# Moving one layer's weight sums out of an attention stage and into the feed-forward stage beside it

## The chip, the core and the metric

The kernel runs on one core of a Trainium2 chip. The time is device microseconds (us) of one execution. A core has a matrix engine (TensorE, in the profile PE, with PEld for its weight loads), three engines for elementwise work (VectorE as DVE, ScalarE as ACT, GpSimd as POOL), an engine that here only issues transfers (SyncE, SP), and 16 DMA engines that move data between the chip's main memory (DRAM) and the on-chip memory (SBUF). TensorE writes into PSUM, a separate memory of eight banks. Each engine runs its own instructions strictly in order, and so does each queue of transfers that an engine issues: an instruction that waits holds up all that stands behind it.

## What is computed

The input x has two batches of 2048 tokens of 256 features. The output is x plus an attention plus a feed-forward network (FFN), both on the same normalized input:

```
xn  = layernorm(x)
q, k, v = xn Wq, xn Wk, xn Wv                      # all 256 -> 256
att = softmax(causal(q k^T) / 16) v Wo
h   = silu((xn w1^T) * w1_s) * ((xn w2^T) * w2_s)  # 256 -> 1024
h   = gelu((h h1^T) * h1_s)                        # 1024 -> 1024
h   = gelu((h h2^T) * h2_s)                        # 1024 -> 1024
out = x + att + (h w3^T) * w3_s                    # 1024 -> 256
```

The FFN weights w1, w2, h1, h2 and w3 hold only -1, 0 and 1 in the test's data, and everything is float32.

## The kernel before

**Two stages.** The attention of all tokens comes first, and then the FFN of all tokens. The tokens are cut into eight blocks n of 512, four to a batch. The FFN reads the normalized input, turned so that the features lie on the partitions, from DRAM (xT_d), where the attention stage has put it, and the attention's result from DRAM too (r_d).

**The attention.** A query tile (n, t) is 128 tokens. There are 32 tiles, numbered j = 0 to 31: batch 0 from its last tile (which looks at all 2048 keys) to its first, then batch 1 from its first tile to its last. For precision, each float32 operand is held as a rounded part and a remainder, and a product takes three matmuls. For each block of 512 keys, `score` does 6 matmuls (line 345); VectorE copies the scores out of PSUM and takes their maximum (the scale-and-max instruction, and `low`, line 360); ScalarE takes the exponentials of the whole row (L366). The exponentials have to be turned before they can be multiplied with the values. Short rows are turned by TensorE (`pt`, L410). Long rows are turned "by blocks": VectorE turns 32x32 squares (L236), SyncE's queue stores them to a scratch in DRAM (`d`, L241) and loads them back rearranged (`e`, L248). Then ScalarE rounds them (`pT`, L404), VectorE or GpSimd makes the remainder (L406), and `weigh` multiplies with the values (`po`, L424 and L429).

**The order of the attention.** The program's order is written out by hand. `merged(a, b, beside)` (L43) interleaves two lists of steps, the scores of tile j and the weighing of an earlier tile, by their costs, which are counted in columns that TensorE passes. A row that is turned by blocks is weighed at the earliest 42,000 such columns after its scores (DELAY_BLOCKS), another one 9,000 after. After each step `merged` calls `beside(cost)` (L565), which takes the next piece of background work from a queue once enough columns have passed.

**The background work.** The FFN has a fast path that holds only if the weights are what they are in this data. In it the 1024 x 1024 layers h1 and h2 are computed as 2 x 2 blocks with seven block products in place of eight (the list STEPS), and so need, for each layer, seven weight matrices of 512 x 512: the quarters A11, A12, A22 and four sums S1 to S4. These are made during the attention and put in DRAM (`factors`), and at the same time it is found out whether the weights have the values that the path needs. There are two kinds of background work:

- *Looks* (`look`, L487) at w1, w2 and w3, six in all, of 512 KB each: a load issued by ScalarE, for w1 and w2 a rounding by GpSimd into SBUF, then VectorE masks the low bits and ScalarE sums them into a column of `low_bits`. One is taken before every second tile from j = 3 on.
- *Rounds of factors* (the queue `factoring`, L510 to L560), from tile j = 14 on (FACTORS_FROM), so from shortly before the second batch: four for h1 and four for h2. A round loads two 512 KB chunks c and c+4 of the weight (ScalarE's queue, L521), takes the sign of each (ScalarE, L527), counts where the chunk differs from its sign (VectorE, L529), makes four sums of 128 x 512 (GpSimd, L539), and stores A11, the four sums and A12, A22 (SyncE's queue, L550 to L553, 1.75 MB in all).

The signs and the sums lie in the tile xh0 (1 MB), which is the place of the FFN's first input and is unused until then. So a round's first sign can be written only once the store of the last round's sums has left xh0, and the FFN's first input is loaded (L663, on SyncE's queue) only after the last store. The chunks share two staging buffers (`stgp`).

When the queue is empty, VectorE takes the maximum of `low_bits` (L657), TensorE and VectorE make the flag of it, and after the attention all engines read the flag and take the branch to `ffn_ternary` (L665), or to a slower FFN that holds for all weights.

**The FFN.** It takes the blocks in four pairs (n, n+1). `first(n)` (L696) computes the gated layer: for each of 16 parts of 128 x 512, 8 matmuls (L709), four into each of two banks, a silu by ScalarE into a tile `a` (L714), and a product by VectorE (L716) into `f`. It goes through the quarters B11, B12, B22, B21 and, with `split` (L692 and L693), `t1` and `b22`, makes the right-hand sides of the seven products. `square` does the seven products of a layer (L756), each of 32 matmuls into four banks, after loading their left factor from DRAM (L749, SyncE's queue, three buffers). In the end comes w3 (L847). GpSimd has in this stage one subtraction per part in `b22` (L734), one in `square` (L791) and the sum of x and the attention's result (L837). w3 is loaded at the start of the FFN (L820) and rounded by GpSimd (L131). The banks of PSUM (eight) and the buffers of the pools `raw` (26 of 128 x 512) and `h` (16) are taken in turns.

The functions that the change touches:

Of the kernel before, what the change touches and what calls it, by code (L numbers as in the profile page):

```python
# [32 lines left out]
FACTORS_FROM = 14  # L33
# [29 lines left out]
def attn_ffn_kernel(  # L63
# [72 lines left out]
    def rows(n, t):  # L136
        return ds((n % NB) * TB + t * P, P)

    with ExitStack() as actx:
# [342 lines left out]

        low_bits = cp.tile([P, 32], F32, name="low_bits")
        looked = [0]
        looks = []

        def look(src, dst):  # L487
            def go():
                t = stgp.tile([P, SC], F32, tag="stg", name=f"stg_{looked[0]}")
                nc.scalar.dma_start(out=t, in_=src)  # L490
                if dst is not None:
                    rounded(dst, t)
                tb = t.bitcast(U32)
                with tc.issue_after(marks["DVE"]):
                    nc.vector.tensor_scalar(tb, tb, LOW_BITS, None, ALU.bitwise_and)
                at = low_bits[:, looked[0] : looked[0] + 1]
                nc.scalar.activation(t, tb, AF.Copy, accum_out=at)
                looked[0] += 1

            looks.append(go)  # L500

        for src, dst in ((w1, w1_sb), (w2, w2_sb)):
            for c in range(src.shape[1]):
                look(src[:, c, :], dst[:, c, :])
        for c in range(0, HC, SC // D):
            look(w3[:, c : c + SC // D, :].rearrange("p c d -> p (c d)"), None)

        factoring = []  # L510

        def factor(name, src, c):

            halves = []
            sums = xh0.rearrange("p c h t -> p (c h) t")
            f = factors[name]

            def fetch():
                for k in (c, c + HK):
                    t = stgp.tile([P, SC], F32, tag="stg", name=f"stg_{name}_{k}")  # L520
                    nc.scalar.dma_start(out=t, in_=src[:, k, :])  # L521
                    halves.append(t)

            def compare(i):
                t, sign = halves[i], sums[:, ts(i, 2), :].rearrange("p a o -> p (a o)")
                with tc.issue_after(marks["ACT"]):
                    nc.scalar.activation(sign, t, AF.Sign)  # L527
                with tc.issue_after(marks["DVE"]):
                    nc.vector.scalar_tensor_tensor(  # L529
                        sign, t, 1.0, sign.bitcast(F32), ALU.mult, ALU.not_equal,  # L530
                        accum_out=low_bits[:, looked[0] : looked[0] + 1],
                    )
                looked[0] += 1

            def of(i):
                return halves[i // 2][:, ts(i % 2, HB)]

            def add(out, x, y, op):
                nc.gpsimd.tensor_tensor(sums[:, out, :], x, y, op)  # L539

            def s12():
                add(0, of(1), of(3), ALU.add)
                add(1, sums[:, 0, :].bitcast(F32), of(0), ALU.subtract)

            def s43():
                add(2, of(2), sums[:, 1, :].bitcast(F32), ALU.subtract)
                add(3, of(0), of(1), ALU.subtract)

            def store():
                nc.sync.dma_start(out=f[:, 0, c, :], in_=of(0))  # L550
                nc.sync.dma_start(out=f[:, 1:5, c, :], in_=sums.bitcast(F32))
                nc.sync.dma_start(out=f[:, 5, c, :], in_=of(2))
                nc.sync.dma_start(out=f[:, 6, c, :], in_=of(3))  # L553

            factoring.extend([
                (6000, fetch), (9500, lambda: compare(0)), (2500, lambda: compare(1)),
                (3000, s12), (3000, s43), (3000, store),
            ])

        for name, src in (("h1", h1), ("h2", h2)):  # L560
            for c in range(HK):
                factor(name, src, c)
        since = [0]

        def beside(cost):  # L565
            if j >= FACTORS_FROM:
                since[0] += cost
                if factoring and since[0] >= factoring[0][0]:
                    since[0] = 0
                    factoring.pop(0)[1]()  # L570
# [43 lines left out]
        def before(j):  # L614
# [12 lines left out]
            if j >= 3 and j % 2 and looks:  # L627
                looks.pop(0)()
# [6 lines left out]
        while until < len(tiles) - 1:  # L635
# [17 lines left out]
            if not factoring and not checked:  # L653
                assert not looks
# [10 lines left out]
    def ffn_ternary(actx):  # L665
# [4 lines left out]
        rawp = actx.enter_context(tc.tile_pool(name="rawpt", bufs=26))  # L670
        hp = actx.enter_context(tc.tile_pool(name="hpt", bufs=4 * HK))
        tp = actx.enter_context(tc.tile_pool(name="tpt", bufs=2))
# [23 lines left out]
        def first(n):  # L696
# [3 lines left out]
            for k in ("B11", "B12", "B22", "B21"):  # L700
                xh = xh1 if k[2] == "2" else xh0
                for i in range(HK):
# [3 lines left out]
                    for p, w in ((p1, w1_sb), (p2, w2_sb)):  # L706
# [6 lines left out]
                    g = tp.tile([P, TB], F32, tag="a", name=f"a_{name}")  # L713
                    nc.scalar.activation(g, p1, AF.Silu, scale=sc["w1"][:, o : o + 1])  # L714
                    f = B[k][i] = raw(f"f_{name}")
                    nc.vector.scalar_tensor_tensor(  # L716
                        f, p2, sc["w2"][:, o : o + 1], g, ALU.mult, ALU.mult
# [5 lines left out]
                    elif k == "B22":  # L723
                        b22(B, sets, f"{n}", i)
            return B, sets
# [14 lines left out]
        def square(layer, n, B, sets, last):  # L740
# [5 lines left out]
            def product(step, out, start):  # L746
# [6 lines left out]
                for o in range(HK):  # L753
                    for c in range(HK):
                        for a in range(2):
# [4 lines left out]
                            )  # L760

# [54 lines left out]

        load_xh(1)
        for c in range(0, HC, SC // D):
            t = fw.tile([P, SC], F32, name=f"stgt_{c}")
# [231 lines left out]
```

## Time and profile before

The median of three runs is 897.68 us (897.17 to 897.79). The profiled execution took 901.06 us, of which its span is 899.3 us.

| | busy us | share of the span | instructions |
|---|---|---|---|
| TensorE (PE) | 860.9 | 96% | 4280 |
| VectorE (DVE) | 615.8 | 68% | 1111 |
| ScalarE (ACT) | 498.6 | 55% | 881 |
| GpSimd (POOL) | 257.6 | 29% | 192 |

The DMA engines moved 158.33 MB, 176 GB/s on the mean. The mean granted clock of TensorE was 0.983 of full speed.

The attention runs from 0 to about 303.9 us, the FFN from there to the end. The batches change at about 150 us. A line of the timeline has a start, a duration, the engine, the line of the kernel, the operation, its output and inputs by the program's names, the shapes, and in brackets for how long the engine stood idle before it and what it had waited for. A line of a table by stage has the stretch, its length, then for PE, PEld, DVE, ACT and POOL the busy time and the number of instructions, then the granted clock, the share of the DMA engines' time that was busy, and GB/s. A line of the waits has the engine and instruction that waited, what it waited for, the sum of those waits, their number and the longest.

### The profile page before, as it was taken

To read this page: it belongs to the slowest core of one execution; us is meant where nothing else is said; L and a number is where in the kernel's file an instruction comes from. 1 tells how busy PE (TensorE), PEld (TensorE's weight loads), DVE (VectorE), ACT (ScalarE), POOL (GpSimd) and SP (SyncE) were. 2 spreads that over 40 slices of the span, in tenths; PEclk is the share of its full clock that TensorE was granted. 3 is DMA by queue.
4 is the path that set the end of the run, shared out by engine and by line. 5 is a ranking of instruction groups with operands and counts; after the bars stand their busy time and mean duration, and the time that the engine had idled before them with its cause. 6 is when DMAs were issued, how large, how long until landed. Compare 5 with 4: busy or idle time off the path is not lost.

```text
span 899.3 us, 12302 instructions
## 1 busy us (share of the span) xinstructions
PE 860.9 (96%) x4280; PEld 725.0 (81%) x4280; DVE 615.8 (68%) x1111; ACT 498.6 (55%) x881; POOL 257.6 (29%) x192
## 2 busy tenths in 40 slices
PE   8999999889886899999999999999999999999996
PEld 5988878778674788888988888898888898888886
DVE  6698566777675396596479487649659647948763
ACT  3456465545444356576446576726658644656670
POOL 4022533534346242150026024014315002602401
PEclk8999999999996999999999999999999999999999
DMA  7686698688987754444433444442444443144412
GB/s 251 246 243 203 160 329 290 222 283 291 323 272 242 275 200 153 154 154 141 141 94 141 140 141 141 144 145 90 145 153 154 153 141 95 48 140 141 141 48 74
DMA packets 62838, 158.33 MB, mean 176 GB/s; under 512 B 6576, under 2 KB 36400, under 8 KB 53552
## 3 DMA queue, kind: packets, MB, share of 16 engines
q1 hardware_dynamic: 59024, 144.87, 47.6%
q10 hardware_dynamic: 3744, 12.58, 4.5%
q8 instruction: 36, 0.59, 0.3%
q14 instruction: 34, 0.28, 0.1%
HBM read 109.72 MB, written 47.71 MB: 175 GB/s over the span
## 4 chain that ended last, share of the span: by engine, by line
PE 68%; DMA 16%; POOL 5%; DVE 5%; ACT 2%; SPq 2%; issue 2%; ACTq 0%; POOLq 0%; DVEq 0%
PE ps_h_X L756 26%; PE ps_w_B L709 13%; PE ps_h_Z L756 13%; PE ps_h_Y L756 6%; PE ps_y L847 6%; DMA factors_h<-xh 5%; DMA e<-d 4%; DMA d<-b 4%; POOL xh L539 3%; SPq L248 2%; PE pv L317 1%; PE pss L345 1%; DMA x<-d_x 1%; POOL pT L406 1%; DVE st L219 1%
## 5 line engine op out<-in xcount | busy, mean ns | idle before, releaser
L345 PE MATMUL pss<-k,q 128*128 128x512 f32 (+3 forms) x480 | 110.9, 372 | 3.0 <-DVE q L196 2.1
L345 PEld LDWEIGHTS pss<-k,q 128*128 128x128 f32 x480 | 82.9, 191 | 17.2 <-DVE q L196 2.6
L424 PE MATMUL po<-v,pT 128*128 128x512 f32 x272 | 81.0, 411 | 11.0 <-ACT pT L404 8.8
L756 PE MATMUL ps_h_X<-h_h_T,w_h_S 128*128 128x512 f32 x384 | 89.0, 389 | 0.0
L756 PEld LDWEIGHTS ps_h_X<-h_h_T,w_h_S 128*128 128x128 f32 x384 | 72.1, 188 | 15.0
L837 POOL TENSOR_TENSOR rt<-rt,xt 128x1024 f32<-128x1024 f32 x8 | 19.2, 2400 | 222.7 <-DMA rt<-r_d 203.6
L714 ACT ACTIVATE a_w_B<-ps_w_B,w_s_sb 128x512 f32<-128x512 f32 x64 | 43.1, 684 | 46.8 <-PE ps_w_B L709 44.6
L775 ACT ACTIVATE k_h_u<-k_h_u,h_s_sb 128x512 f32<-128x512 f32 x64 | 46.3, 723 | 40.8 <-DVE k_h_u L774 40.6
L734 POOL TENSOR_TENSOR k_h_u<-k_h_p,k_h_u 128x512 f32<-128x512 f32 x16 | 23.2, 1452 | 147.4 <-ACT h_h_B L692 130.8
L424 PEld LDWEIGHTS po<-v,pT 128*128 128x128 f32 x272 | 48.5, 195 | 19.5 <-ACT pT L404 10.3
L709 PE MATMUL ps_w_B<-xh,w_sb 128*128 128x512 f32 x256 | 61.3, 398 | 2.8 <-DMA xh<-xT_d 2.8
L366 ACT ACTIVATE s<-s,low 128x1024 f32<-128x1024 f32 (+7 forms) x48 | 42.9, 896 | 36.0 <-DVE low L360 34.2
L847 PEld LDWEIGHTS ps_y<-w_sbt,h_h_B 128*128 128x128 f32 x512 | 62.0, 192 | 0.3
L847 PE MATMUL ps_y<-w_sbt,h_h_B 128*128 128x256 f32 x512 | 62.1, 283 | 0.0
L709 PE MATMUL ps_w_B<-xh1t,w_sb 128*128 128x512 f32 x256 | 60.6, 396 | 0.0
L709 PEld LDWEIGHTS ps_w_B<-xh,w_sb 128*128 128x128 f32 x256 | 48.9, 192 | 13.4 <-issue 3.0
L756 PE MATMUL ps_h_Y<-h_h_B,w_h_A 128*128 128x512 f32 x256 | 59.3, 389 | 0.0
L756 PE MATMUL ps_h_X<-h_h_T,w_h_A 128*128 128x512 f32 x256 | 59.3, 389 | 0.0
L406 POOL TENSOR_TENSOR pT<-e,pT 128x512 fp32r<-128x512 f32 (+3 forms) x30 | 35.5, 1185 | 77.6 <-ACT pT L404 68.0
L709 PEld LDWEIGHTS ps_w_B<-xh1t,w_sb 128*128 128x128 f32 x256 | 48.2, 188 | 11.7
L756 PEld LDWEIGHTS ps_h_Y<-h_h_B,w_h_A 128*128 128x128 f32 x256 | 48.0, 188 | 10.0
L756 PEld LDWEIGHTS ps_h_X<-h_h_T,w_h_A 128*128 128x128 f32 x256 | 48.0, 188 | 10.0
(135 smaller groups left out, 1865.7 us busy)
## 6 DMA issues: line engine op xcount, KB each, us to landing
w_h_S<-factors_h SPq DMA_DIRECT2D x32, 1024.0 KB, 4.8
w_h_A<-factors_h SPq DMA_DIRECT2D x24, 1024.0 KB, 4.8
d<-b SPq DMA_DIRECT2D x18, 512.0 KB, 3.9
e<-d SPq DMA_DIRECT2D x72, 128.0 KB, 4.4
xT_d<-k SPq DMA_DIRECT2D x8, 1024.0 KB, 4.9
stg_h<-in_ffn_h_w ACTq DMA_DIRECT2D x16, 512.0 KB, 6.5
factors_h<-xh SPq DMA_DIRECT2D x8, 1024.0 KB, 8.3
factors_h<-stg_h SPq DMA_DIRECT2D x24, 256.0 KB, 5.1
```

The lines of the kernel that those rows point to most:

```text
L345: nc.tensor.matmul(out=ps[:, :w], lhsT=qs[n][:, c, a, ts(t, P)], rhs=ks[m][:, c, b, :w], start=(k == 0), stop=(m < n and k == 3 * DC - 1),)
L366: marks["ACT"] = nc.scalar.activation(st["s"][:, at], st["s"][:, at], AF.Exp, bias=low, accum_out=st["sums"][:, u // UK : u // UK + 1],).ins
L406: engine.tensor_tensor(lo, src, hi.bitcast(F32), ALU.subtract)
L424: nc.tensor.matmul(out=st["po"], lhsT=pT[:, 0, ts(j, P)], rhs=vs[m][:, j, :, :], start=(m == first and j == 0), stop=False,)
L539: nc.gpsimd.tensor_tensor(sums[:, out, :], x, y, op)
L709: nc.tensor.matmul(out=p, lhsT=w[:, c, ts(o, P)], rhs=xh[:, c, a, :], start=(c == 0 and a == 0), stop=(c == DC - 1 and a == 1),)
L714: nc.scalar.activation(g, p1, AF.Silu, scale=sc["w1"][:, o : o + 1])
L734: nc.gpsimd.tensor_tensor(B["B12"][i], B["B22"][i], B["B12"][i], ALU.subtract)
L756: nc.tensor.matmul(out=out[o], lhsT=w[:, c, ts(o, P)], rhs=sets[right][c][:, a, :], start=(start and c == 0 and a == 0), stop=(c == HK - 1 ...
L775: nc.scalar.activation(C[k][o], r[o] if r else banks[o], AF.Gelu, scale=s[:, at : at + 1])
L837: nc.gpsimd.tensor_tensor(rest, rest, xt, ALU.add)
L847: nc.tensor.matmul(out=ys[t][:, :D], lhsT=h[c][:, a, ts(t, P)], rhs=w3_sb[:, c, :], start=(c == 0 and a == 0), stop=(c == HC - 1 and a == 1),)
```

## The change

The sums of h1 are made in the attention as before. The sums of h2 are made in the FFN beside the first pair of blocks. All comparisons, those of h2 too, stay in the attention, since the flag depends on them.

- One queue `looks` takes the place of the two kinds of background work. It is emptied through `beside` from tile j = 3 on (LOOKS_FROM). Its order: four looks at w1 and w2; then four times a round for h1 (two loads, two comparisons, four sums, the stores) and two comparisons for h2 without sums or stores; then two looks at w3. In TensorE columns it is 330,000 long, in 56 steps. The store of the sums is issued ahead of those of the quarters.
- In the FFN a list `later` holds four `make_h2(c)` and two `load_w3`. `make_h2` loads two chunks of h2 again (SyncE's queue), makes four sums on GpSimd in a tile of its own, and issues four stores. The four are taken after the quarters B11 and B12 of `first(0)` and after the products 0 and 2 of h1's first `square`; the two `load_w3` after products 4 and 5.
- To make room, the tile `a` goes (the silu is written into `f`, which VectorE then multiplies in place), and `raw` has 25 buffers in place of 26.

```diff
-FACTORS_FROM = 14
+LOOKS_FROM = 3
...
+    def sums_of_factors(sums, halves, which):
+
+        (a11, a21), (a12, a22) = ((t[:, :HB], t[:, HB:]) for t in halves)
+        done = sums.bitcast(F32) if sums.dtype == F32R else sums
+        for i in which:
+            x, y, op = (
+                (a21, a22, ALU.add),
+                (done[:, 0, :], a11, ALU.subtract),
+                (a12, done[:, 1, :], ALU.subtract),
+                (a11, a21, ALU.subtract),
+            )[i]
+            nc.gpsimd.tensor_tensor(sums[:, i, :], x, y, op)
+
+    def store_factors(f, c, sums, halves):
+        nc.sync.dma_start(out=f[:, 1:5, c, :], in_=sums)
+        nc.sync.dma_start(out=f[:, 0, c, :], in_=halves[0][:, :HB])
+        for i in range(2):
+            nc.sync.dma_start(out=f[:, 5 + i, c, :], in_=halves[1][:, ts(i, HB)])
...
-            looks.append(go)
+            looks.extend([(6000, lambda: fetched_weights(src, got)), (9000, bits)])
...
+        def look_signs(src):
+            got = []
+            looks.extend([
+                (6000, lambda: fetched_weights(src, got)),
+                (9000, lambda: compare(got[0], looked[0] % 2)),
+            ])
+
+        def look_and_factor(src, f, c):
+            got = []
+            looks.extend([
+                (6000, lambda: fetched_weights(src[:, c, :], got)),
+                (2000, lambda: fetched_weights(src[:, c + HK, :], got)),
+                (8000, lambda: compare(got[0], 0)),
+                (2500, lambda: compare(got[1], 1)),
+                (3500, lambda: sums_of_factors(sums, got, (0, 1))),
+                (4000, lambda: sums_of_factors(sums, got, (2, 3))),
+                (4000, lambda: store_factors(f, c, sums.bitcast(F32), got)),
+            ])
...
+        for c in range(HK):
+            look_and_factor(h1, factors["h1"], c)
+            for k in (2 * c, 2 * c + 1):
+                look_signs(h2[:, k, :])
...
-            factoring.extend([
-                (6000, fetch), (9500, lambda: compare(0)), (2500, lambda: compare(1)),
-                (3000, s12), (3000, s43), (3000, store),
-            ])
-
-        for name, src in (("h1", h1), ("h2", h2)):
-            for c in range(HK):
-                factor(name, src, c)
...
-            if j >= FACTORS_FROM:
+            if j >= LOOKS_FROM:
...
-            if j >= 3 and j % 2 and looks:
-                looks.pop(0)()
...
-        rawp = actx.enter_context(tc.tile_pool(name="rawpt", bufs=26))
+        stgp = actx.enter_context(tc.tile_pool(name="stgpt", bufs=2))
+        rawp = actx.enter_context(tc.tile_pool(name="rawpt", bufs=25))
...
-                    g = tp.tile([P, TB], F32, tag="a", name=f"a_{name}")
-                    nc.scalar.activation(g, p1, AF.Silu, scale=sc["w1"][:, o : o + 1])
                     f = B[k][i] = raw(f"f_{name}")
+                    nc.scalar.activation(f, p1, AF.Silu, scale=sc["w1"][:, o : o + 1])
                     nc.vector.scalar_tensor_tensor(
-                        f, p2, sc["w2"][:, o : o + 1], g, ALU.mult, ALU.mult
+                        f, p2, sc["w2"][:, o : o + 1], f, ALU.mult, ALU.mult
                     )
...
+                if later and k in ("B11", "B12"):
+                    later.pop(0)()
...
+                if later and step in (0, 2, 4, 5):
+                    later.pop(0)()
...
+        def make_h2(c):
+            halves = []
+            for k in (c, c + HK):
+                t = stgp.tile([P, SC], F32, tag="stg", name=f"stgt_h2_{k}")
+                nc.sync.dma_start(out=t, in_=h2[:, k, :])
+                halves.append(t)
+            sums = stgp.tile([P, 4, HB], F32, tag="sums", name=f"sums_h2_{c}", bufs=1)
+            sums_of_factors(sums, halves, range(4))
+            store_factors(factors["h2"], c, sums, halves)
+
+        def load_w3(c):
+            t = stgp.tile([P, SC], F32, tag="stg", name=f"stgt_w3_{c}")
+            nc.sync.dma_start(out=t, in_=w3[:, c : c + SC // D, :].rearrange("p c d -> p (c d)"))
+            rounded(w3_sb[:, c : c + SC // D, :].rearrange("p c d -> p (c d)"), t)
```

## The prediction

> **What bounds the kernel now.** I read the page first, then a table of the span by stage, then what TensorE (PE) waits for, then the timeline around the longest wait. The page, its engine rows:
>
> ```profile
> span 899.3 us, 12302 instructions
> PE 860.9 (96%) x4280; PEld 725.0 (81%) x4280; DVE 615.8 (68%) x1111; ACT 498.6 (55%) x881; POOL 257.6 (29%) x192
> ```
>
> PE is busy 96% of the span, so the whole kernel holds some 38 us of PE idle. The table by stage (busy us of each engine, granted clock, DMA share, GB/s) says where it lies:
>
> ```profile
> 0.00:150.00 150.00, 142.96 (x776) 120.04 (x776) 104.56 (x288) 74.88 (x149) 47.49 (x68) 0.98 0.79 248
> 150.00:260.00 110.00, 99.95 (x542) 85.19 (x543) 81.61 (x211) 58.29 (x119) 54.14 (x38) 0.98 0.78 267
> 260.00:303.90 43.90, 30.07 (x149) 24.59 (x147) 20.58 (x37) 17.66 (x31) 17.84 (x14) 0.84 0.75 259
> 303.90:452.20 148.30, 148.30 (x705) 124.86 (x706) 102.35 (x139) 88.54 (x147) 35.85 (x20) 0.99 0.48 168
> ```
>
> The first pair of the FFN (last row) has no PE idle at all; the three rows of the attention have 7.0, 10.1 and 13.8 us. The last 44 us before the FFN are the worst, and there the clock is down to 0.84 as well. What PE waits for in the attention:
>
> ```profile
> PE po L424 <- ACT pT L404: 8.8, 5, 4.5
> PE pt L410 <- ACT s L366: 6.1, 1, 6.1
> ...
> PE po L424 <- DVE r L443: 2.2, 1, 2.2
> ```
>
> The 6.1 us is one wait. Its timeline:
>
> ```profile
> 266.61 2.00 ACT L527 ACTIVATE xh<-stg_h 128x1024 fp32r<-128x1024 f32 x2 [2.67 <-DMA factors_h<-xh]
> 267.76 1.23 DVE L529 SCALAR_TENSOR_TENSOR xh<-stg_h,xh 128x1024 fp32r<-128x1024 f32 x1 [3.14 <-ACT xh L527]
> ...
> 272.27 1.15 ACT L366 ACTIVATE s<-s,low 128x1024 f32<-128x1024 f32 x1 [3.29 <-DVE low L360]
> ...
> 273.56 1.97 PE L410 MATMUL pt<-ident,s 128*128 128x128 f32 x8 [6.14 <-ACT s L366]
> ```
>
> The reader is to see a line of queues: ACT's sign of an h2 chunk (L527) waits until the store of the previous sums has left xh0; VectorE (DVE) stands behind it at the comparison (L529) and can't copy scores or find their maximum; ACT then waits for that maximum before its exponentials; PE waits for those. The factor work is off the path by its busy time and on it by its waits. The same stage ends thus:
>
> ```profile
> 303.90 2.39 PE L709 MATMUL ps_w_B<-xh,w_sb 128*128 128x512 f32 x7 [2.78 <-DMA xh<-xT_d]
> ```
>
> xh0 is the scratch of the sums, so the FFN's first input is fetched only after the last sums are stored (store issued at 294.74, fetch at 298.94).
>
> **The change, part by part.** Durations are of the profiled execution: 901.06 us, its span 899.3, 1.76 around it. It stands 3.38 us above the median of the runs shown, 897.68; I carry differences over to the median.
>
> (1) *The tail, 260 to 303.9.* The queue of looks is now 330,000 cost units long: 4 looks at w1 and w2 of 15,000, four times h1's round of 30,000 with two h2 comparisons of 15,000, 2 looks at w3 of 15,000. A score block of 6 matmuls is 3,072 units; at 0.23 us a matmul (7.25 us for 32 in the FFN) that is 2,200 units per us. The 56 steps overshoot by some half block each, 84,000 units: 414,000 units, 188 us of PE work from tile 3, whose first operation (L219) stands at 53. So the queue is empty at about 250, and the changed program has the fetch of xh0 ahead of the last tiles' transposing loads and the flag ahead of the last tile but one. What was late in the tail: 13.8 us of PE idle; busy 30.07 us at 0.84 of the clock, up to 0.16 x 30.07 = 4.8 us; and a slow ramp of the FFN, whose first 128 matmuls take 31.41 us against 29.57 in the next pair, 1.8 us. Bounds: 0 (something else is late at once) to -20.5. Next late is the turn of a score row through DRAM, d 3.9 us and e 4.4 us by the DMA rows; the order has 12 us of other PE work between. I keep 3.8 of the idle, half of the clock loss and most of the ramp: -10 - 2.5 - 1 = **-13.5**.
>
> (2) *Factor rounds elsewhere.* Before, six of eight rounds end by 260 (their sums leave for DRAM at 163, 180, 218, 258 and between), with 10.1 us of idle in 150 to 260: 1.7 us a round. After, four rounds remain, 6.7 us, plus eight lone h2 comparisons, a sign (ACT, 1.05 us) and a compare (DVE, 1.37 us) each without sums or stores: between 0 and four rounds' 6.7, I take 2.2, nearer 0 because what stalls is the store that the sign waits for. Against 10.1: **-1.1**, ends -3.4 and +3.3. Each h2 round that leaves takes four POOL sums (1.57 us mean) and four stores on SP (1.75 MB) along; its two loads on ACT's queue stay for the comparison.
>
> (3) *The first batch, 53 to 150.* It gets what leaves the second: some two rounds and four comparisons, 8 loads of 0.5 MB and 3.5 MB of stores, less 1 MB for w3. That is 6.5 MB on top of 23.7 MB in 97 us, 311 GB/s where the busiest 10 us of the attention moved 376. PE idles 2.7 us there now. Behind a wait of ACT for a store stand the exponentials and the casts of pT; behind a store on SP stand the transposing loads e. Ends: 0, all of it in gaps, and +8, two rounds at what the worst round costs (4.1 us, the longest of ACT's waits for that store). I take **+2**.
>
> (4) *The FFN's first pair.* Added: per chunk 2 loads, 4 stores (24 more on SP in all, 0.32 to 0.44 us of issue each) and 4 POOL sums; w3's two loads and roundings come later. SP: the products' weights (L749) stand behind stores that wait for POOL. The first three are issued ahead of any such wait. The fourth can't start before product 0 frees its buffer, and by the order waits for sums that are ready some 40 us into the stage; it is needed at 53 (31.4 + 3 x 7.25), a load takes 4.8 us: hidden. h2's first factors are needed some 82 us in; the last sums are done at about 63 and stored 8.3 us later. w3 is needed at 133. POOL against DVE is not hidden so well. Alone, an operation of DVE on 512 elements with two SBUF inputs takes 0.69 us; beside POOL it takes longer:
>
> ```profile
> 324.03 2.50 DVE L693 TENSOR_TENSOR h_T<-f_w_B,h_T 128x512 fp32r<-128x512 f32 x1
> 326.45 0.74 DVE L716 SCALAR_TENSOR_TENSOR f_w_B<-ps_w_B,w_s_sb,a_w_B 128x512 f32<-128x512 f32 x1
> 327.11 1.12 DVE L693 TENSOR_TENSOR h_B<-f_w_B,h_B 128x512 fp32r<-128x512 f32 x1
> ```
>
> ```profile
> 323.58 2.40 POOL L837 TENSOR_TENSOR rt<-rt,xt 128x1024 f32<-128x1024 f32 x1 [9.16 <-ACT h_T L692]
> 325.93 5.16 POOL L734 TENSOR_TENSOR f_w_B<-f_w_B,f_w_B 128x512 f32<-128x512 f32 x3
> ```
>
> During the three POOL operations from 325.93 DVE needed 5.2 us for 3.5 us of work: 0.55 lost per sum; by the row of twice the width 1.8, so 0.9. DVE is full from 319 to 344, and the eight sums of chunks 0 and 1 fall into that stage: 8 x 0.55 = 4.4, less 1.6 for the two roundings that leave it (2.96 us for two splits of 0.69). The slack is 1.2 us: the second bank of product 0 is wanted at 337.1 and its DVE read ended at 335.9. So **+1.6**, ends 0 and 8 x 0.9 - 2.8 = +4.4.
>
> The trace has DVE reads from PSUM untouched (0.74) and SBUF pairs stretched. The Trainium skill, "SBUF — State Buffer", section "SBUF: two separate sides", speaks harder against this change: the port pair that VectorE and GpSimd share is an exclusive lock held for the whole instruction, and the loser fully blocks. By that rule each sum of 1.45 us would stop DVE for all of its length, 11.6 - 2.8 = +8.8 instead of +1.6. The row, where other DVE work runs meanwhile, decides.
>
> (5) *Edits that cost nothing:* silu written into f and multiplied in place keeps count and shapes, and drops ACT's wait for the two buffers (1.8 us in all, PE not behind it); 25 raw buffers for 26, as a square holds at most 24 at once. If that cover is wrong ACT's copies wait, at 0.59 us each.
>
> Sum: -13.5 - 1.1 + 2 + 1.6 = **-11.0**: 890.1 for the profiled execution, 886.7 on the median's scale.
>
> **Rivals.**
> - *It ends slower: the first batch takes it back.* ACT and SP are blocked by rounds while the DMA engines are 0.8 full. For: the whole of 100 to 150 stands near a DMA share of 1.0. Against: before, PE idles 2.7 us there in spite of it, and work stands 19 us ahead (42,000 units of delay at 2,200 a us). Price: four rounds at the longest wait (4.1), 16.4, in place of the 2 in the sum: -11 + 14.4 = +3.4, about 901. It decides once a round costs over 3.3 us of PE.
> - *DVE is the FFN's new bound.* POOL's sums stop DVE for +4.4 or more and term 1 is halved: about 893. For: DVE 5.00 of 5 us in that stretch; against: the PSUM reads that free the banks don't slow.
> - *The tail stays late for another reason:* the round trip through DRAM takes the place of the factors' waits, as po waits for pT (4.5 us once) and behind that for e. Term 1 is then -5: about 895.
> - *It does nothing:* the queue lasts to the end as before and only order changes. Only if PE stalls stretch it by 40 us; within 0.2%.
>
> **How the numbers follow.** Forecast 0.54, first rival 0.21, second 0.10, third 0.10, none 0.05. Forecast: 886.7, its own range 879 to 892 by term 1 between -19 and -8. Faster by over 0.2% (1.8 us, about what a measurement of this kernel can tell from no change): 0.54 + 0.10 + 0.10 less 0.02 = 0.72; slower 0.21; within 0.07. The range goes from 877 (term 1 in full, term 4 at nothing) to 902, just over the first rival's price, leaving out under 2 in 10.
>
> **What would show it.** Right: no PE wait above 3 us between 260 and the FFN and no factor work after 255; the FFN starting within 1 us of the last po matmul; xh0 not waited for; 8 of the 16 sums beside full DVE, with product 0 a microsecond or two late. Wrong: ACT waiting for stores of sums between 100 and 200 with PE behind it, or PE idle in 304 to 340.

## The result, and the profile after

The changed kernel takes 885.05 us (median of four runs, 883.69 to 889.26), against 897.73 for the kernel before: the ratio is 0.9867, with a 95% interval of 0.9834 to 0.9901. So it is faster by 12.7 us, where 11.0 were predicted. The profiled execution took 885.32 us, 15.7 less than that of before, which stood 3.3 us above its own median. The differences below are those of the two profiled executions.

The engine rows of the changed kernel's page:

```profile
span 883.4 us, 12258 instructions
PE 855.4 (97%) x4280; PEld 721.5 (82%) x4280; DVE 621.6 (70%) x1111; ACT 498.1 (56%) x881; POOL 258.4 (29%) x192
```

The table of stages of the changed kernel (length, busy time of PE, PEld, DVE, ACT and POOL, granted clock, DMA share, GB/s). The FFN's first pair now begins at 285.62:

```profile
0.00:150.00 150.00, 139.50 (x755) 116.80 (x756) 110.44 (x299) 77.23 (x148) 58.55 (x73) 0.98 0.79 246
150.00:260.00 110.00, 107.95 (x598) 92.84 (x597) 82.82 (x217) 64.61 (x131) 31.22 (x26) 1.00 0.87 281
260.00:285.62 25.62, 20.98 (x116) 17.98 (x114) 9.35 (x22) 9.56 (x19) 4.31 (x4) 0.93 0.31 94
285.62:433.92 148.30, 145.50 (x689) 121.54 (x690) 111.30 (x138) 87.75 (x147) 59.66 (x35) 1.00 0.70 248
```

Read row by row against the table before: TensorE's idle time rises from 7.0 to 10.5 us up to 150, falls from 10.1 to 2.0 between 150 and 260, and from 13.8 to 4.6 in the rest of the attention. The FFN's first pair, which had none, has 2.8. What TensorE still waits for in the changed kernel:

```profile
PE po L443 <- ACT pT L423: 5.8, 4, 3.4
PE pss L364 <- ACT q L214: 2.4, 1, 2.4
PE ps_h_X L763 <- DVE f_w_B L721: 2.2, 1, 2.2
PE ps_w_B L715 <- DVE r L462: 1.3, 1, 1.3
...
PE ps_h_Y L763 <- DMA w_h_A<-factors_h: 0.6, 1, 0.6
```

The wait of 6.1 us for the exponentials and the 2.8 for xh0 are gone. ScalarE's sign waits less for the store of the last sums; the same row before had 17.8 us in 6 waits:

```profile
ACT xh L537 <- DMA factors_h<-xh: 5.7, 3, 4.1
```

The longest wait left, 3.4 us, is in the end of the attention. Its timeline, by ScalarE, SyncE's queue and TensorE:

```profile
256.34 1.03 ACT L385 ACTIVATE s<-s,low 128x896 f32<-128x896 f32 x1
...
259.43 0.48 SPq L260 DMA_DIRECT2D d<-b  x1
260.43 4.75 SPq L267 DMA_DIRECT2D e<-d  x6
...
267.13 0.62 ACT L423 CAST pT<-e 128x512 fp32r<-128x512 f32 x1 [6.87 <-DMA e<-d]
...
267.80 0.50 PE L443 MATMUL po<-v,pT 128*128 128x512 f32 x1 [3.36 <-ACT pT L423]
```

This is the plain round trip of a score row through DRAM: exponentials at 256.3, store at 259.4, loads from 260.4, rounding at 267.1. No factor work stands in it: the last sign ran at 236.6, and the flag's matmul at 251.1.

### The profile page after: what moved, and what is told of

The parts are those of the page before. It is cut to its first block, busy times and chain, and to the rows that moved or that the text cites. A ratio compares the mean times of both kernels' runs of the same rounds, so it can differ in the third digit from the quotient of the medians.

```text
span 883.4 us, 12258 instructions
## 1 busy us (share of the span) xinstructions
PE 855.4 (97%) x4280; PEld 721.5 (82%) x4280; DVE 621.6 (70%) x1111; ACT 498.1 (56%) x881; POOL 258.4 (29%) x192
## 4 chain that ended last, share of the span: by engine, by line
PE 61%; DMA 4%; DVE 1%; POOL 1%; issue 0%; SPq 0%; POOLq 0%; DVEq 0%
PE ps_h_X L763 26%; PE ps_h_Z L763 13%; PE ps_w_B L715 10%; PE ps_h_Y L763 7%; PE ps_y L871 6%; DMA xt<-in_attn_x 2%; DMA w_h_A<-factors_h 1%; POOL rt L861 1%; DMA rt<-r_d 0%; DVE f_w_B L742 0%; DVE h_B L699 0%; POOL f_w_B L741 0%; DMA out<-yt 0%; DVE yt L878 0%; DVE yt L877 0%
## 5 line engine op out<-in xcount | busy, mean ns | idle before, releaser
L720 ACT ACTIVATE f_w_B<-ps_w_B,w_s_sb 128x512 f32<-128x512 f32 x64 | 43.0, 684 | 42.5 <-PE ps_w_B L715 42.5
```

What stands on the lines that cost most here:

```text
L720: nc.scalar.activation(f, p1, AF.Silu, scale=sc["w1"][:, o : o + 1])
```

## The clock, which a wait takes along

One thing has to be told before the sum is made. The trace's clock records show TensorE at half clock in stretches of 3.4 us or a multiple of it, each behind a wait. Leaving out one at each kernel's start and one that its end cuts off, they begin at these times. Before: 236.7 (3.4 us long), 270.9 (6.8), 284.5 (6.8) and 305.0 (3.4). After: 128.3 and 268.3, 3.4 us each. A stretch of 3.4 us costs some 1.7 us if TensorE has work in it. The difference of the two executions then adds up:

| | us |
|---|---|
| 0 to 53: no difference in idle time, but 3.4 us less at half clock, which comes at the kernel's start in other kernels too | -1.7 |
| 53 to 150: idle 2.7 to 6.2, and a half-clock stretch | +5.2 |
| 150 to 260: idle 10.0 to 2.0, and one half-clock stretch less | -9.7 |
| 260 to the FFN: idle 13.8 to 4.6 (-9.2); half clock 13.7 to 3.4 us, in which TensorE stood idle for 4.6 anyway: (10.2 - 4.6) / 2 = 2.8 | -12.0 |
| the FFN's start without the half-clock stretch at 305.0 | -1.7 |
| the rest of the FFN, which lasts 597.8 in place of 595.4 | +4.1 |
| sum | -15.8 |

The measured difference of the spans is -15.9.

A kernel made for this measures the price of a wait in the FFN, where TensorE otherwise has no gap. It puts pairs of small matmuls in, the second of which waits for a chain of copies by ScalarE:

```diff
+        def pause(k, name):
+            g = raw(f"pause_{name}")
+            b = banks(f"pause_{name}", 2)
+            nc.tensor.matmul(out=b[0], lhsT=xh0[:, 0, 0, :P], rhs=xh0[:, 0, 0, :], start=True, stop=True)
+            nc.scalar.copy(g, b[0])
+            for _ in range(k):
+                nc.scalar.copy(g, g)
+            nc.tensor.matmul(out=b[1][:1, :1], lhsT=g[:, :1], rhs=g[:, 1:2], start=True, stop=True)
...
+            if n:
+                pause((0, 0, 1, 3)[n // 2], f"a{n}")
             B, sets = first(n)
...
+                if m == n:
+                    pause((2, 5, 8, 0)[n // 2], f"b{n}")
```

> The changed kernel with six waits of different length put into the FFN, where TensorE is otherwise busy without a gap and at full clock: a small matmul, k copies by ScalarE one after the other, and a matmul that waits for them, ahead of the FFN's pairs 2, 3, 4 (k = 0, 1, 3) and in the middle of the last layer of pairs 1, 2, 3 (k = 2, 5, 8); 1 to 6 us by 0.59 us a copy. If a wait costs only itself: 20 us in all or so, the clock stays at 1.0. If a wait brings half clock with it, as it seems in the attention (2.4 us: 3.4 us at half; 4.5 and 6.1 us: 6.8 us each): short ones nothing, those above about 2.3 us another 1.7 to 3.4 us each, 8 us more.

There are seven waits, not six: the last pair has one of k = 0 too. One execution took 909.31 us, its span 907.4. The first six in its timeline, in brackets:

```profile
429.57 0.19 PE L849 MATMUL ps_pause_b<-pause_b 128*1 128x1 f32 x2 [1.97 <-ACT pause_b L848]
440.02 0.19 PE L849 MATMUL ps_pause_a<-pause_a 128*1 128x1 f32 x2 [0.67 <-ACT pause_a L846]
583.37 0.19 PE L849 MATMUL ps_pause_b<-pause_b 128*1 128x1 f32 x2 [3.92 <-ACT pause_b L848]
594.48 0.19 PE L849 MATMUL ps_pause_a<-pause_a 128*1 128x1 f32 x2 [1.32 <-ACT pause_a L848]
739.79 0.19 PE L849 MATMUL ps_pause_b<-pause_b 128*1 128x1 f32 x2 [5.87 <-ACT pause_b L848]
752.50 0.19 PE L849 MATMUL ps_pause_a<-pause_a 128*1 128x1 f32 x2 [2.62 <-ACT pause_a L848]
```

And its table of stretches around the first of them (the granted clock is the third number from the end):

```profile
426.40:429.80 3.40, 1.43 (x13) 1.07 (x12) 0.85 (x2) 1.82 (x3) 0.00 (x0) 1.00 0.29 89
430.00:433.40 3.40, 3.40 (x18) 3.40 (x17) 0.00 (x0) 0.00 (x0) 0.50 (x1) 0.50 0.47 146
433.40:436.80 3.40, 3.40 (x31) 3.40 (x30) 1.52 (x4) 0.00 (x0) 1.88 (x1) 1.00 0.15 16
```

From 430.0 to 433.4, TensorE does 18 matmuls where the next stretch does 31. It counts as busy throughout: the busy share can't show this, only the clock can. Lined up matmul by matmul with the changed kernel, the delay grows behind the 1.97 us wait by another 1.6 us, behind the 3.92 by 1.6, behind the 5.87 by 1.9 (6.8 us at half clock, of which the wait itself fills 2.6), and behind 0.67, 1.32 and 2.62 by less than 0.1. So a wait of about 2 us or more can cost itself and some 1.6 to 1.9 us on top. The 1.97 is below the 2.3 that was expected as the least. Its length alone does not decide: the 2.62 drew nothing; and the wait of 2.2 us for product 0 drew none in the changed kernel's profile, while the same wait, 2.1 us here, was followed by 3.4 us at half clock from 317.4.

What decides can be read from the clock records. In each of the fourteen profiles the half-clock stretches begin whole multiples of 3.413 us apart, so the span can be divided into slots of that length. Leave out the first 16 us, where less was enough. Of the other slots up to TensorE's last instruction 3475 are at full clock, and 41 of these are followed by half clock. They are exactly those in which TensorE stood idle for 1.80 us or more; the most idle of the rest has 1.78. The 1.97 and the 2.1 of this kernel fell into one slot each. The 2.62 was divided between two slots, 0.98 and 1.64 us, and the 2.2 of the changed kernel into 0.44 and 1.75. Once at half clock, a slot with 0.62 us of idle time or more was always followed by another. Counted from the kernel's start, the first slot border stood at 2.0 us in one execution of the changed kernel and at 0.1 in another, so which wait is cut in two differs between executions.

## Experiments on the cause

*Two halves of the change, each alone.* Theory A is that spreading the work does it, so that the queue is empty before the last tiles; theory B, that the h2 sums have to leave the attention. The first kernel keeps them there, in the new queue (each ratio below is to runs of the kernel before on the same chip):

```diff
         for c in range(HK):
             look_and_factor(h1, factors["h1"], c)
-            for k in (2 * c, 2 * c + 1):
-                look_signs(h2[:, k, :])
+            look_and_factor(h2, factors["h2"], c)
...
-        later = [lambda c=c: make_h2(c) for c in range(HK)]
+        later = []
```

> The changed kernel, but h2's four full rounds stay in the attention (in the one queue from tile 3, in the place of h2's lone comparisons, the queue as long as before, 330,000 units), and the FFN makes no sums of h2. Theory A, the spreading does it (the queue is empty before the last tiles, xh0 and the exponentials of the end wait for nothing): the tail keeps its gain, the first batch pays for twice as many rounds (another +2 to +4 on the +4 seen between 68 and 155 us), the FFN gets back the 2.2 us that product 0 waited: 885 to 888. Theory B, the h2 sums have to leave the attention because VectorE, the shared scratch and the DMA engines can't carry eight rounds: most of the gain is gone, 892 to 898, with sign operations waiting for stores and TensorE idle behind them.

Measured: 882.89 us, ratio 0.9874 (0.9835 to 0.9912); four of its six runs took 881.0 to 883.1, two 890.6 and 890.8. The second has the old queue at its old places, from tile 14 on, and makes only h2's sums and stores in the FFN:

```diff
-LOOKS_FROM = 3
+LOOKS_FROM = 14
...
+        for c in range(HK):
+            factor(h1, factors["h1"], c, True, 0)
+        for c in range(HK):
+            factor(h2, None, c, False, 9000 if c else 0)    # loads and comparisons only
```

> The changed kernel, but with the queue of the kernel before: looks at w1, w2, w3 before every second tile, rounds from tile 14 on, h2's comparisons at the same costs and places as before; only h2's sums and stores are gone from there and are made in the FFN. Theory A (spreading does it): the signs and comparisons of h2 still come in the last 40 us and xh0 is free only at the end, so a part of the tail stays: 889 to 894. Theory B (the sums' stores and GpSimd's sums were what the signs waited for): the waits of the sign for a store are gone with the stores, and with them the 6.1 and 4.5 us of TensorE: 882 to 887, since the first batch stays at its old speed.

Measured: 886.08 us, ratio 0.9871 (0.9842 to 0.9901). Each half alone gives the whole gain, within what can be told; they don't add. The same stages in the kernel that only spreads:

```profile
53.00:150.00 97.00, 91.46 (x485) 78.00 (x484) 74.48 (x200) 56.67 (x112) 44.57 (x43) 0.95 0.82 254
150.00:260.00 110.00, 108.64 (x606) 94.63 (x605) 88.40 (x215) 62.66 (x126) 56.16 (x42) 0.99 0.96 326
260.00:286.98 26.98, 22.19 (x121) 18.90 (x119) 8.89 (x21) 11.10 (x22) 4.60 (x4) 0.87 0.41 131
```

and in the one that only moves:

```profile
53.00:150.00 97.00, 95.64 (x529) 82.38 (x528) 69.94 (x193) 53.89 (x111) 34.18 (x37) 1.00 0.77 240
150.00:260.00 110.00, 102.70 (x560) 88.10 (x559) 85.32 (x215) 63.23 (x125) 42.69 (x30) 0.98 0.81 268
260.00:288.40 28.40, 24.31 (x128) 19.98 (x127) 13.76 (x30) 13.20 (x26) 5.97 (x5) 0.94 0.46 145
```

The first pays in the first batch (5.5 us idle, against 1.4) and has almost no idle in the second (1.4, against 7.3). Both have some 4 to 5 us left in the end, where the kernel before had 13.8. So it is the end that both mend, one by having nothing there, the other by having less there: its last sign begins at 261.0 and its last comparison at 263.7, but its last sums are stored at 220.9.

*The end of the queue alone.* If that is the cause, one number in the kernel before should do:

```diff
-FACTORS_FROM = 14
+FACTORS_FROM = 6
```

> The kernel before with one number changed: the rounds start at tile 6 instead of 14, so that the queue is empty some 40 us earlier. All eight rounds with sums and stores stay in the attention. Theory A (what counts is only that the queue ends well before the last tiles): 882 to 887, no TensorE wait above 3.6 us after 260, the first batch some 5 us later. Theory B (the h2 sums have to go, or the spacing of the new queue is what helps): 890 to 896.

Measured: 911.27 us, ratio 1.0145 (1.0125 to 1.0165), slower than before. TensorE's timeline and a row of its stages say why:

```profile
232.66 0.40 PE L429 MATMUL po<-v,pT 128*128 128x256 f32 x2
243.36 0.19 PE L659 MATMUL pf<-ones,most 128*1 128x1 f32 x2 [10.30 <-DVE most L657]
243.48 6.18 PE L345 MATMUL pss<-k,q 128*128 128x512 f32 x18
```

```profile
234.40:248.10 13.70, 4.74 (x13) 3.74 (x14) 3.40 (x8) 2.00 (x2) 5.94 (x4) 0.50 0.44 157
```

The matmul of the flag is put into TensorE's program where the queue becomes empty, and that is now in the middle of the attention, with the last quarter of the scores behind it in order. It waits 10.3 us for the last comparisons, and 13.7 us at half clock come with it. A check that hides at the end of a stage is a barrier in its middle. The wait and its half clock make 12.6 of the 24.1 us by which this kernel's span is longer than that of the next one. Waits of 9.7 us in all between 205 and 232 go too when the flag moves; why was not traced. So the flag was moved to the end:

```diff
-            if not factoring and not checked:
+            if not factoring and not checked and until == len(tiles) - 1:
```

> The kernel before with its rounds from tile 6 on, as in the run that took 911, but the maximum of the comparisons and the flag are made after the last tile. In that run TensorE's order had the flag's matmul ahead of four tiles of scores, and waited 10.3 us for it; here it stands after the last scores again. If the early end of the rounds was right and only the flag's place was wrong: 882 to 888, as with all eight rounds in the changed kernel's queue. If it is the spacing of the new queue that helps, or the sums that have to go: 891 to 897.

Measured: 884.64 us, ratio 0.9857 (0.9828 to 0.9887): the whole gain of the change from two short edits, with all eight rounds, the old queue's costs and the old FFN. The store of its last sums is issued at 254.7, against 294.7 in the kernel before. Its stages:

```profile
53.00:150.00 97.00, 92.86 (x512) 78.89 (x511) 79.26 (x201) 55.21 (x110) 49.24 (x47) 1.00 0.84 267
150.00:260.00 110.00, 105.44 (x568) 90.98 (x567) 82.61 (x211) 64.20 (x128) 47.58 (x36) 0.97 0.91 309
260.00:288.34 28.34, 23.06 (x129) 19.81 (x128) 9.44 (x20) 10.50 (x20) 4.63 (x4) 0.94 0.48 137
```

This settles theory A as far as it says that an early end is enough. It does not make it the only remedy, as the kernel that only moves shows.

*The queue later, or longer.* Two kernels shift the changed kernel's queue back towards the end. The first starts it at tile 8, with 0.7 of the costs:

```diff
-LOOKS_FROM = 3
+LOOKS_FROM = 8
...
-                if looks and since[0] >= looks[0][0]:
+                if looks and since[0] >= 0.7 * looks[0][0]:
```

> The changed kernel, but the queue starts at tile 8 instead of 3 and each step's cost is 0.7 of what it was, so that it ends at about the same place. If the 5 us that the changed kernel loses between 68 and 155 us come from rounds in the first batch's busy part: 880 to 883, with TensorE's waits near 96 to 109 us gone. If the rounds cost the same wherever they are, or more when they stand closer: 885 to 890.

Measured: 892.25 us, ratio 0.9949 (0.993 to 0.9969). The idle time in the first batch fell (3.4 us), but 150 to 260 had 7.3 and the end 5.9; the sign waited 14.0 us for stores, against 17.8 before. That is above both expectations. The rounds here stand later and closer at once, and which of the two costs more than the first batch got back is not told apart. The second has every cost times 1.15:

```diff
-                if looks and since[0] >= looks[0][0]:
+                if looks and since[0] >= 1.15 * looks[0][0]:
```

> The changed kernel with every step's cost times 1.15, so that its queue reaches into the last tiles again, as in the kernel before; h2's sums stay in the FFN. Theory A (the end of the queue): much of the gain goes again, 890 to 895, with xh0 or the flag late at the FFN's start and TensorE's waits in the last 30 us longer than the 3.4 of the changed kernel. Theory B (the sums and stores that left): 883 to 887.

Measured: 892.69 us, ratio 0.9945 (0.9924 to 0.9966; twelve runs from 887.28 to 897.55). The time is what theory A expected, but the trace does not show its reason. Signs ended at 259.7, xh0 was not waited for, and the end had 5.2 us of idle, hardly more than the changed kernel. What it lost lies at other places: a wait of 6.4 us at 105.7 for the rounded scores and one of 3.1 at 171.8, each with a half-clock stretch of 6.8 us at it. A shift of the same steps makes others collide, and no theory here says which.

*The changed kernel once more*, beside these:

> The changed kernel itself, so that the kernels beside it are compared with it on the same chip. Both theories: 884 to 886, as recorded.

Measured: 885.52 us, ratio 0.9862 (0.984 to 0.9884).

*The price of the sums in the FFN.* In the profiled kernels that make all of h2's sums there, the FFN lasts 596.7 to 599.6 us, 597.8 and 598.0 in the changed kernel. With all rounds in the attention it lasts 594.3 in the kernel that only spreads, 593.6 and 594.1 in the two that start at tile 6; the exception is 597.0, in the kernel below that spreads and turns two tiles by TensorE, where 1.8 us more lie behind TensorE's last instruction. One kernel makes only the first of the four chunks' sums:

```diff
-            sums_of_factors(sums, halves, range(4))
-            store_factors(factors["h2"], c, sums, halves)
+            if c == 0:
+                made.append(stgp.tile([P, 4, HB], F32, tag="sums", name=f"sums_h2_{c}", bufs=1))
+                sums_of_factors(made[0], halves, range(4))
+            store_factors(factors["h2"], c, made[0], halves)
```

> The changed kernel with GpSimd's sums of h2 left out for three of the four chunks (h2's factors then hold the first chunk's sums); loads and stores stay. If GpSimd beside VectorE is the FFN's price: the first product starts 30 us after the FFN's start instead of 32, no wait of the second bank, 882 to 883.5. If it is SyncE's queue: no change, 885.

Measured: 881.99 us, ratio 0.9808 (0.9779 to 0.9837), with an FFN of 594.9 us. So most of the price hangs on GpSimd's sums. SyncE's queue kept its loads and stores, but its stores no longer wait for three chunks' sums, and the wait of 0.6 us for a weight load is gone too; that part of the queue is not told apart. The wait of TensorE for VectorE falls from 2.2 to 0.8 us. In the changed kernel it looks so. VectorE and GpSimd beside the first four sums, which run from 294.22 to 300.63:

```profile
293.67 0.74 DVE L721 SCALAR_TENSOR_TENSOR f_w_B<-ps_w_B,w_s_sb,f_w_B 128x512 f32<-128x512 f32 x1
...
294.22 1.30 POOL L150 TENSOR_TENSOR sums_h<-stgt_h 128x512 f32<-128x512 f32 x1 [18.57 <-DMA stgt_h<-in_ffn_h_w]
294.44 3.32 DVE L699 TENSOR_TENSOR h_B<-f_w_B,h_B 128x512 fp32r<-128x512 f32 x2
...
295.47 1.74 POOL L150 TENSOR_TENSOR sums_h<-stgt_h,stgt_h 128x512 f32<-128x512 f32 x1
...
297.29 1.63 POOL L150 TENSOR_TENSOR sums_h<-sums_h,stgt_h 128x512 f32<-128x512 f32 x1
297.69 0.74 DVE L721 SCALAR_TENSOR_TENSOR f_w_B<-ps_w_B,w_s_sb,f_w_B 128x512 f32<-128x512 f32 x1
298.46 1.01 DVE L736 TENSOR_TENSOR f_w_B<-f_w_B,f_w_B 128x512 f32<-128x512 f32 x1
299.00 1.63 POOL L150 TENSOR_TENSOR sums_h<-stgt_h,sums_h 128x512 f32<-128x512 f32 x1
...
300.16 1.01 DVE L736 TENSOR_TENSOR f_w_B<-f_w_B,f_w_B 128x512 f32<-128x512 f32 x1
```

Four operations with two SBUF inputs take 5.34 us in place of 4 x 0.69: 2.6 us lost to four sums, 0.65 each. Those that read PSUM stay at 0.74. The two engines take turns: the operation from 298.46 ends at 299.47, 0.55 us after the sum from 297.29 does (298.92), and the next sum ends at 300.63, 1.16 us after that. In the changed kernel's profile all eleven VectorE operations with two SBUF inputs that begin during a sum end 0.55 us after it, whatever was left of it. Where VectorE is full, the end of it comes out on TensorE, the second bank of product 0:

```profile
314.20 1.73 POOL L150 TENSOR_TENSOR sums_h<-stgt_h 128x512 f32<-128x512 f32 x1
314.71 1.77 DVE L699 TENSOR_TENSOR h_B<-f_w_B,h_B 128x512 fp32r<-128x512 f32 x1
...
317.01 0.74 DVE L721 SCALAR_TENSOR_TENSOR f_w_B<-ps_w_B,w_s_sb,f_w_B 128x512 f32<-128x512 f32 x1
...
317.80 1.43 PE L763 MATMUL ps_h_X<-h_B,w_h_A 128*128 128x512 f32 x5 [2.19 <-DVE f_w_B L721]
```

*Attempts at something faster.* The 3.4 us wait is the round trip of the last but one tile, so that tile was turned by TensorE too:

```diff
-            return min(UK, kt - u) >= LEAST and (n, t) != (N - 1, NT - 1)
+            return min(UK, kt - u) >= LEAST and (n, t) not in ((N - 1, NT - 1), (N - 1, NT - 2))
```

> The changed kernel, but the last two query tiles, not only the last, are turned by TensorE instead of through DRAM. If the 3.4 us wait at 264 us is the round trip of that tile through DRAM and the half clock behind it (3.4 us at 0.5, so 1.7 us) hangs on it: -5.1, plus 15 transposes of 0.12 us (+1.8), together 881 to 883. If the tile before it, which still goes through DRAM, is late in its place: 885 to 888.

Measured: 883.32 us, ratio 0.9841 (0.9822 to 0.986), which overlaps with the changed kernel's intervals. The wait was gone (0.7 us in its place), and the end's idle fell to 2.0 us. The same in the kernel that only spreads:

> All eight rounds in the attention from tile 3 on, none in the FFN (which ran 2 to 3 us shorter without them), and the last two tiles turned by TensorE (which took away the 3.5 us wait near 262 us and the 6.8 us of half clock behind it, for 1.8 us of transposes). If both hold together: 878 to 881, faster than both kernels. If another wait takes the place: 882 to 884.

Measured: 885.33 us, ratio 0.9857 (0.9836 to 0.9878): no better than either. TensorE's last instruction is followed by 9.7 us here and 9.3 in the kernel above, 7.9 in the changed one. The last attempt makes two of h2's rounds in each place (the FFN's after products 0 and 2) and holds the second of the FFN's behind GpSimd's other work:

```diff
+            if c < HK // 2:
+                look_and_factor(h2, factors["h2"], c)
+            else:
+                for k in (c, c + HK):
+                    look_signs(h2[:, k, :])
...
+            with tc.issue_after(after_t4[0]) if c == HK - 1 else ExitStack():
+                sums_of_factors(sums, halves, range(4))
...
-        later = [lambda c=c: make_h2(c) for c in range(HK)]
+        later = [lambda c=c: make_h2(c) for c in range(HK // 2, HK)]
```

> The changed kernel with three changes: two of h2's four rounds are made in the attention, two in the FFN; the second of these is held back until GpSimd has done its subtractions for h1's products, so that none of its sums lies beside the full VectorE; and the last two tiles are turned by TensorE. The FFN's wait of 2.2 us before the second bank of product 0 should go, and the 3.4 us wait near 264 us with its half clock: 880 to 882.5, faster than the changed kernel. If the extra two rounds or the turning cost as much elsewhere: 884 to 886.

Measured: 888.22 us, ratio 0.9886 (0.9862 to 0.9911), slower than the changed kernel by its median. The extra rounds cost the first batch (8.7 us idle), and four sums beside VectorE were still followed by a wait of 1.6 us, for a bank of the gated layer 28.9 us into the FFN.

## Why the prediction was right, point by point

The time, 885.05, is 1.65 us off the forecast of 886.7, inside its own range. That it is so near is luck. Between the profiled executions, 890.1 was forecast and 885.3 measured, so the sum was off by 4.7: term 2 by -8.6 and the kernel's start, which had no term, by -1.7, set off in part by term 3 (+3.2) and term 4 (+2.5). Another 3.1 us falls away because the kernel before's profiled execution stood further above its median (3.4 by the forecast's median) than that of the changed kernel does (0.3).

- *Bound and place* were right: the wait of 6.1 us hung on the line sign, store, comparison, maximum, exponentials; without late rounds it goes. In the 4.5 us wait the signs, behind a store, stand ahead of the rounding of pT on ScalarE:

```profile
283.21 2.00 ACT L527 ACTIVATE xh<-stg_h 128x1024 fp32r<-128x1024 f32 x2 [1.21 <-DMA factors_h<-xh]
285.32 1.14 ACT L404 CAST pT<-e 128x512 fp32r<-128x512 f32 x2
```

- *(1) The tail*, -13.5: measured -13.7. The queue was empty at 251, as worked out (about 250). The idle kept is 4.6, where 3.8 was put; the clock gave 2.8 and the FFN's ramp 1.7, where 2.5 and 1.0 were put. Both are the same thing, half clock behind a wait, and were priced as if they were apart from the waits.
- *(2) Rounds elsewhere*, -1.1, ends -3.4 and +3.3: measured -9.7, far outside. The step that failed is the pricing of a round by the average idle of its stage (1.7 us), and the charge of all four of h1's rounds to 150 to 260. The changed kernel stores their sums at 114.5, 150.0, 182.7 and 222.3: two stand in the first batch, as term 3 itself had assumed. With two rounds the term would have been 3.4 + 2.2 - 10.1 = -4.5. The rest is the price: 150 to 260 has 2.0 us of idle in the changed kernel, and 1.4 with all eight rounds in the new queue, so rounds as such cost little there. Why they cost 10.0 before isn't settled. TensorE's order differs from kernel to kernel, not only in the steps that were moved, and the early start with the old costs has 4.6.
- *(3) The first batch*, +2, ends 0 and +8: measured +5.2, so a mis-sized term; 3.5 of it is idle, 1.7 is clock. That the rounds cause it is shown by the kernel that has none there: 1.4 us idle. The longest wait stands behind two signs, which begin at 125.39 after 1.3 us of waiting for a store, and the rounding of q that follows them:

```profile
128.29 1.22 PE L364 MATMUL pss<-k,q 128*128 128x512 f32 x2 [2.36 <-ACT q L214]
```

- *(4) The FFN's first pair*, +1.6, ends 0 and +4.4: measured +4.1, a mis-sized term. The place was right to the bank, 2.2 us there; 0.6 more is a weight load that was said to be hidden, 0.5 lies behind TensorE's last instruction, and 0.8 is not traced to a place. A sum costs VectorE 0.65 us (0.55 to 0.9 was said). The rows agree with the rule of the Trainium skill's "SBUF — State Buffer", section "SBUF: two separate sides", that one engine has the shared ports for a whole instruction and the other is blocked: the 0.55 us above. The 8.8 us that the prediction made of it did not come. An operation of VectorE lost what was left of the sum when it began, and not the sum's whole length; reads of PSUM lost nothing; and the sums were held up in turn, so that 6.4 us of sums took 2.6 from VectorE.
- *(5)* The edits at nothing show no wait of their own.

Of the rivals, the first batch did take back, but 5.2 and not 16.4. That VectorE becomes the FFN's bound came true, at the price that was named for it (4.4), but without the halved tail. The DRAM round trip is what is left of the tail: a wait above 3 us, which the forecast said would not be there. Both signs of being wrong showed too, each at a small price: ScalarE at a store with TensorE behind it (2.4 us) and TensorE idle early in the FFN (2.2 us). What no step asked is whether the sums had to be moved at all; they hadn't.

## What to carry to other kernels

When background work is late at the end of a stage, try its starting point first: here one number, with the check that depends on it kept at the end, was worth as much as a rewrite that moved half the work and paid some 4 us for it elsewhere. A small instruction that joins a queue's end to an in-order engine must be placed by hand when the queue's end moves. A wait of TensorE brings 1.6 to 1.9 us of half clock on top when 1.8 us of it fall into one slot of 3.4 us, so price waits of about 2 us or more higher than their length, and don't price rounds of work by the mean idle of the stage that they stand in.

## What the hardware showed that was not expected

Half clock comes in stretches of 3.4 us and its multiples (3.4, 6.8, 13.7), and TensorE counts as fully busy in them once its wait is over. It follows a slot of 3.413 us with 1.80 us of idle time or more, so a wait of 1.97 us in an otherwise gapless stage was enough, and one of 2.62 us, cut in two by a border, was not. An operation of VectorE with two SBUF inputs and a sum of GpSimd take turns: each that began during a sum ended 0.55 us after it. One kernel's runs lay 10.3 us apart (887.28 to 897.55), where the kernel before spans 6.1 on the same chip. More or fewer half-clock stretches from run to run would account for a part: the fastest of these runs had a mean clock of 0.987, the slowest 0.982, which is 11.5 and 16.1 us of lost clock over their spans, 4.6 of the 10.3.
